# A small Pool memset behind each transfer of the landing-paced spreads in a four-layer mixture-of-experts kernel

## The chip, the cores and the metric

The kernel runs on 1 core of a Trainium2 chip. The metric is the device time of one launch in microseconds (us), given as the median of several runs; a profile of one further execution supplies the trace. The engines are TensorE (PE in the profile; PEld is its weight load), VectorE (DVE), ScalarE (ACT), GpSimd (POOL) and SyncE (SP, which here only issues transfers). Each has its own instruction stream and works it off in order. They wait for one another, and for transfers, by semaphores.

## The reference, cut to what matters

x has 4 sequences of 1024 tokens with 128 features, float32. It passes through four layers, each an attention-like mix and a feed-forward part, each with a residual and a layer norm behind it:

```python
x = L0_attn_x
x = _layernorm(x + _L0_attn_ref(x, ...))
x = _layernorm(x + _L0_ffn_ref(x, ...))     # a linear layer on block-quantised values
x = _layernorm(x + _L1_attn_ref(x, ...))    # a state-space mix
x = _layernorm(x + _L1_ffn_ref(x, ...))     # 16 experts, 4 for a token, and a shared one
x = _layernorm(x + _L2_attn_ref(x, ...))    # causal attention, 16 heads of 8
x = _layernorm(x + _L2_ffn_ref(x, ...))     # 8 experts, 2 for a token
x = _layernorm(x + _L3_attn_ref(x, ...))    # a Toeplitz mix, gated
x = _layernorm(x + _L3_ffn_ref(x, ...))     # 32 experts, 4 for a token, and a shared one
```

What matters here are the three expert parts. A router gives each token its k experts with a weight each:

```python
topk_scores, topk_idx = jax.lax.top_k(scores, TOPK)
...
h = silu(flat @ gate_w[e]) * (flat @ up_w[e])      # of each chosen expert e
expert_out = h @ down_w[e]
out = sum over the chosen e of expert_out * topk_scores
```

## The kernel before, in words

x stays on the chip in 32 tiles of 128 tokens. The kernel doesn't compute all experts for all tokens: it sorts the tokens by expert into lists in the chip's DRAM, in these steps.

- **Positions** (`positions`, L1261). For a set of tokens and a layer, DVE works out each token's row in the list for each of its choices (`pos`, L1302), so that every expert's rows stand together.
- **Spread** (`spread`, L1374). For each tile of 128 tokens and each choice, POOL issues one indirect transfer (L1327, in `indirect`) that writes the tile's 128 rows of 512 bytes to their places in the list. The lists are named by layer and set: l1r is layer 1's second list (64 transfers), l2a, l2m and l2n are layer 2's lists (32, 16, 16), l3a is layer 3's first (64). In the profile the list's own name has a letter more: l1rr, l2ra, l2rm, l2rn, l3ra.
- **Experts.** For each group of four tiles of a list, SP loads the rows (`gathered`, L1392: xg); this load waits until all transfers of that list have landed. PE transposes them (L169; the copies out are L171 on ACT and L173 on DVE, as hT for the hidden values) and multiplies (L161); DVE multiplies the two branches (L1569) and copies the result out (yg, L1589), and SP stores it to an output list (L1590).
- **Collect** (`collect`, L1439). POOL gathers each token's k results from the output list (yt, again L1327), and DVE adds them to x with their weights (L1452).

Every indirect transfer, scatter or gather, is queued on POOL behind the one before it (`self.moved`), so POOL works them off in one fixed order. Some spreads and collects are "spaced" (`spaced`, L1364): in them each transfer also waits until the transfer two before it has landed (`before`, L1346). All spreads named above are spaced. The first list of layer 1 and the two later lists of layer 3 are not; they issue their transfers without such waits.

The order between the engines' streams is set when the program is built. Parts of the kernel are generators that yield an estimated cost, and `mix` interleaves a main part with a side part by these costs; `self.now`, `self.step` and `self.moved_by` keep the planner's clock. Around the change, from `all` (L1966), the order is:

1. Layer 2's attention for the first half of its rows, with the route and spread of l1r beside it.
2. The experts and the shared expert of l1r, with layer 2's weights loading and the route and spread of l2a beside them. The weights of the shared expert lie in buffers that xg uses later.
3. Layer 2's experts on l2a, with the collect of l1r (64 gathers) beside them.
4. Layer 2's attention for the other half. Beside it: the collect of l2a, layer 3's mix and route for its first set, and the spread of l3a, into which those of l2m and l2n are put when their rows are ready. l3a is issued as 32 transfers, then l2n's 16, then 32 more; l2m's 16 come before.
5. Layer 2's experts on l2m; then on l2n, with the collect of l2m (16 gathers, list l2ym) beside them. These gathers stand behind the last transfers of l3a on POOL.
6. Layer 3's shared part and experts, with the rest beside them.

The functions the diff touches:

Of the kernel before, what the change touches and what calls it, by code (L numbers as in the profile page):

```python
# [20 lines left out]
P = 128  # L21
# [35 lines left out]
class Part:  # L57
# [3 lines left out]
    def __init__(self, name, q0, nq, rows=None, lg0=None):  # L61
        self.name, self.q0, self.nq, self.lg0 = name, q0, nq, lg0
        if rows is None:
            self.order = list(range(q0 * QT, (q0 + nq) * QT))
        else:
            self.order = [tile_of(b, 2 * q + k) for b in rows for q in range(q0, q0 + nq) for k in range(2)]
        self.t0, self.nt = q0 * QT, len(self.order)
# [7 lines left out]
class Kernel:  # L75
    def __init__(self, ctx, tc, ins, out, cols, consts, rows):
        self.tc, self.nc, self.ins, self.out = tc, tc.nc, ins, out
        self.count = itertools.count()
        nc = self.nc
        self.const = self.pool(ctx, "const")  # L80
        self.small = self.pool(ctx, "small", 3)
        self.routes = self.pool(ctx, "routes")
        self.side = self.pool(ctx, "side", 2, space=PSUM)
        dram = self.pool(ctx, "dram", space=DRAM)

        self.cols_t = self.load(self.const, ins["cols"])
        self.cst_t = self.load(self.const, ins["consts"])
        self.x = self.tile(self.const, [P, NT, D], "x")
        self.xT = self.tile(self.const, [P, NT * P], "xT")
        nrow = ins["rows"].shape[1]  # L90
        self.rows_t = self.tile(self.const, [P, nrow], "rows")
        nc.gpsimd.dma_start(out=self.rows_t, in_=ins["rows"].to_broadcast([P, nrow]))
        self.col = {k: self.cols_t[:, a:b] for k, (a, b) in cols.items()}
        self.cst = {k: self.cst_t[:, a:b] for k, (a, b) in consts.items()}
        self.row = {k: self.rows_t[:, a:b] for k, (a, b) in rows.items()}
        self.ident = self.cst["ident"]
        self.eps = self.tile(self.const, [P, 1], "eps")
        nc.vector.memset(self.eps, LN_EPS)
        self.halfpi = self.tile(self.const, [P, 1], "halfpi")
        nc.vector.memset(self.halfpi, math.pi / 2)  # L100
        self.ones = self.tile(self.const, [P, E3], "ones")
        nc.vector.memset(self.ones, 1.0)
        self.rnd = self.tile(self.const, [P, 1], "rnd")
        nc.vector.memset(self.rnd, RND)
        self.drop = self.tile(self.const, [P, 1], "drop")
        nc.vector.memset(self.drop, -RND)
        self.zero = self.tile(self.const, [P, D], "zero")
        nc.gpsimd.memset(self.zero, 0.0)
        self.flag = self.tile(self.const, [1, 1], "flag", I32)
        self.hm = self.tile(self.const, [P, 4], "hmg")  # L110

        self.first, self.rest = Part("a", 0, 2), (Part("b", 2, 1), Part("c", 3, 1))
        self.parts = (self.first, *self.rest)
        self.by_rows = (
            Part("a", 0, 2, range(B), 0), Part("m", 2, 2, (0, 1), NT // 2), Part("n", 2, 2, (2, 3), 3 * NT // 4)
        )

        self.rows_done = 0

        self.listed = set()  # L120

        self.traced, self.latest = nc.cur_bb.bb.instructions, {}
        self.now = self.moved_by = 0.0
        self.moved = []
        self.landing = []
        self.spacing = None

        self.lists, self.route = {}, {}
        self.both = (self.first, Part("r", 2, 2))
        for lay, ne, k in (("l1", E1, K1), ("l2", E2, K2), ("l3", E3, K3)):  # L130
            for pt in {"l1": self.both, "l2": self.by_rows, "l3": self.parts}[lay]:
                tl = -(-((pt.nt * P * k + (P - 1) * ne) // P) // 4) * 4
                self.lists[lay, pt.name] = (
                    self.tile(dram, [tl * P, D], f"{lay}r{pt.name}"), self.tile(dram, [tl * P, D], f"{lay}y{pt.name}"), tl
                )
        self.wall2 = self.tile(dram, [P, E2 * 3 * F2], "wall2")
        self.xsave = self.tile(dram, [P, NT, D], "xsave")

        self.ksave = self.tile(dram, [P, B, BLK], "ksave")
        self.vsave = self.tile(dram, [P, B, 4, (NH + 1) * VW], "vsave")  # L140
# [1232 lines left out]
    def spread(self, lay, part, k):  # L1373

        pos, _, _, done, _ = self.route[lay + part.name]
        rows = self.lists[lay, part.name][0]
        for t in range(part.nt):
            for i in range(k):
                ins = self.indirect(
                    apart=done,  # L1380
                    out=rows, out_offset=bass.IndirectOffsetOnAxis(ap=pos[:, t, i : i + 1], axis=0),
                    in_=self.x[:, part.order[t], :], in_offset=None,
                )
                done.append(ins)
            yield (self.step * k,)
        self.listed.add(lay + part.name)

# [835 lines left out]
```

## Time and profile before

| | us |
|---|---|
| median of 3 runs | 1932.44 (1931.96 to 1936.04) |
| the profiled execution | 1937.33 |
| its span in the trace | 1935.5 |
| PE busy | 1541.5 |
| DVE busy | 1199.2 |
| ACT busy | 900.6 |
| POOL busy | 690.3 |

The granted clock of TensorE over this execution is 0.896 of full speed.

In the profile, a row of a timeline gives the start, the busy time, the engine, the line, the operation with what it writes and reads, how often it ran in a row, and in brackets the engine's idle time before it and what ended that. A row of a group gives the busy time in sum and the mean of one instruction in ns, then the idle time before the group's instructions and its causes. In the windows, each stretch has the busy time of PE, PEld, DVE, ACT and POOL (with instruction counts), then the granted clock, the share of time in which DMA engines worked, and GB/s. L numbers are lines of the kernel before. SPq is SP's queue.

### The profile page before, as it was taken

The page shows a single profiled execution, that of the slowest core. Times are in us where ns is not written, and L with a number is a line of the kernel's source. Part 1 is how long each engine was busy: PE and PEld are TensorE (multiplying, and loading weights), DVE is VectorE, ACT ScalarE, POOL GpSimd, SP SyncE. Part 2 cuts the span into 40 slices and gives each one's busy share as a digit, 9 for nine tenths or more (in the row PEclk, how much of TensorE's full clock was granted, in tenths as well). Part 3 has the DMA queues.
Part 4 walks back from the last instruction along what each step waited for, and adds up shares of the span by engine and source line. Part 5 has one row for each costly group of instructions (what it writes and reads, how often), then busy time and mean ns, then how long its engine had stood idle before and what let it go on. Part 6 is the DMA issues. An engine that isn't in the chain of part 4 may idle for free. (4 is left out here: it accounts for less than half of the span.)

```text
span 1935.5 us, 27095 instructions
## 1 busy us (share of the span) xinstructions
PE 1541.5 (80%) x9025; PEld 920.8 (48%) x9025; DVE 1199.2 (62%) x3491; ACT 900.6 (47%) x1349; POOL 690.3 (36%) x670
## 2 busy tenths in 40 slices
PE   7885677597847887989977878798798998999850
PEld 3332433385423345856632232333355757768650
DVE  8998698465766664635564565546442446866383
ACT  5876265243324554423336756564532236644330
POOL 2000148604630660265443000030536430567775
PEclk9897688798978998999988988898988999989985
DMA  9990002244430113632241000000452213425452
GB/s 297 288 288 10 1 17 86 87 126 133 159 129 18 60 63 129 183 96 73 78 137 32 1 1 1 2 23 1 159 213 83 66 28 93 141 68 167 122 147 61
DMA packets 215530, 187.10 MB, mean 97 GB/s; under 512 B 16528, under 2 KB 194064, under 8 KB 214864
## 3 DMA queue, kind: packets, MB, share of 16 engines
q1 hardware_dynamic: 194672, 142.29, 23.6%
q0 software_dynamic: 20704, 42.86, 7.3%
q8 instruction: 84, 1.38, 0.3%
q14 instruction: 70, 0.57, 0.1%
HBM read 88.49 MB, written 96.60 MB: 96 GB/s over the span
## 5 line engine op out<-in xcount | busy, mean ns | idle before, releaser
L1081 ACT ACTIVATE pr<-sc 128x1024 f32<-128x1024 f32 x288 | 279.4, 1021 | 175.2 <-PE sc L161 174.8
L161 PE MATMUL sc<-qm,kT 32*128 32x512 f32 (+3 forms) x1536 | 197.7, 559 | 16.7 <-ACT pr L1081 16.7
L161 PE MATMUL s<-pr,va 128*32 128x512 f32 (+3 forms) x1536 | 167.5, 532 | 19.0 <-DVE x L1019 10.2
L161 PE MATMUL gu<-ld,xgT 128*128 x640 | 165.1, 400 | 10.2 <-DVE hg L1812 5.9
L1087 DVE TENSOR_TENSOR pr<-pr,ld 128x512 f32<-128x512 f32 (+1 forms) x160 | 91.7, 581 | 105.6 <-ACT pr L1081 105.4
L161 PE MATMUL gu<-wall,xgT 128*128 x304 | 148.2, 612 | 2.0 <-ACT xgT L171 2.0
L161 PEld LDWEIGHTS sc<-qm,kT 32*128 32x128 f32 x1536 | 83.7, 194 | 112.4 <-issue 61.1
L161 PEld LDWEIGHTS gu<-ld,xgT 128*128 128x128 f32 x640 | 119.5, 198 | 34.7 <-DVE hg L1812 6.1
L1812 DVE TENSOR_TENSOR hg<-sg,gu 128x256 f32<-128x256 f32 x160 | 66.0, 417 | 92.0 <-ACT sg L1811 91.6
L173 DVE COPY hT<-tp 128x512 f32<-128x512 f32 x118 | 80.9, 686 | 66.2 <-PE tp L169 66.2
L1567 ACT ACTIVATE sg<-gu 128x512 f32<-128x512 f32 x76 | 45.4, 597 | 144.7 <-PE gu L161 143.6
L1811 ACT ACTIVATE sg<-gu 128x256 f32<-128x256 f32 x160 | 61.3, 385 | 107.7 <-PE gu L161 79.8
L171 ACT COPY xgT<-tp 128x512 f32<-128x512 f32 x99 | 58.0, 586 | 99.9 <-PE tp L169 99.8
L1327 POOL DMA_INDIRECT l1ra<-x,posl1a x64 | 79.8, 1246 | 61.3 <-DVE peq L1321 42.0
L1327 POOL DMA_INDIRECT l1rr<-x,posl1r x64 | 65.4, 1022 | 100.9 <-DVE posl1r L1302 70.8
L169 PEld LDWEIGHTS tp<-ld,hg 128*128 128x128 f32 x624 | 77.4, 141 | 49.0 <-issue 32.5
L1569 DVE TENSOR_TENSOR hg<-sg,gu 128x512 f32<-128x512 f32 x76 | 51.8, 682 | 78.9 <-ACT sg L1567 78.8
L1327 POOL DMA_INDIRECT l2rm<-x,posl2m x16 | 15.7, 983 | 236.8 <-DVE peq L1320 230.1
L169 PE MATMUL tp<-ld,hg 128*128 128x128 f32 x624 | 96.4, 275 | 3.7 <-DVE hg L1812 2.0
L1327 POOL DMA_INDIRECT l3ra<-x,posl3a x64 | 63.7, 996 | 93.3 <-DVE usedl3a L1315 51.0
L161 PEld LDWEIGHTS s<-pr,va 128*32 128x32 f32 x1536 | 37.1, 113 | 122.6 <-issue 78.4
L161 PE MATMUL yp<-ld,hT 128*128 x640 | 86.1, 276 | 2.3 <-DVE mv L197 1.5
(447 smaller groups left out, 3439.1 us busy)
## 6 DMA issues: line engine op xcount, KB each, us to landing
wall<-wall SPq DMA_DIRECT2D x16, 768.0 KB, 7.8
l3ra<-zero SPq DMA_DIRECT2D x1, 6144.0 KB, 25.5
ld<-in_l_w SPq DMA_DIRECT2D x2, 3072.0 KB, 10.6
wall<-we SPq DMA_DIRECT2D x24, 256.0 KB, 2.1
ld<-in_l_w SPq DMA_DIRECT2D x1, 6144.0 KB, 20.6
l1ra<-zero SPq DMA_DIRECT2D x1, 5120.0 KB, 19.6
l1rr<-zero SPq DMA_DIRECT2D x1, 5120.0 KB, 23.1
xg<-l3ra SPq DMA_DIRECT2D x20, 256.0 KB, 2.9
```

What stands on the lines that cost most here:

```text
L161: return self.nc.tensor.matmul(out, lhsT, rhs, start=start, stop=stop)
L169: nc.tensor.transpose(pt[:, k * P : (k + 1) * P], s, self.ident)
L171: nc.scalar.copy(dst, pt[:, : n * P])
L173: nc.vector.tensor_copy(dst, pt[:, : n * P])
L1081: nc.scalar.activation(pr, sc[h], AF.Exp)
L1087: nc.vector.tensor_tensor(d, d, cst["tril"].unsqueeze(1).unsqueeze(1).to_broadcast([P, 2, n, P]), ALU.mult)
L1327: ins = self.nc.gpsimd.indirect_dma_start(**kw)
L1567: nc.scalar.activation(sg, gu[:, 0, :], AF.Silu)
L1569: nc.vector.tensor_tensor(h, sg, gu[:, 1, :], ALU.mult)
L1811: nc.scalar.activation(sg, pg[:, :, 0, :], AF.Silu)
L1812: nc.vector.tensor_tensor(h[:, 2 * c : 2 * c + 2, :], sg, pg[:, :, 1, :], ALU.mult)
```

## The change

One tile of 128x384 bytes is added to the constants, and in `spread`, when the spread is spaced, a memset of it on POOL follows each indirect transfer. The memset is ordered behind the transfer on POOL's stream and entered in `self.moved`, so that the next indirect transfer is ordered behind the memset. It doesn't wait for the transfer's landing, and nothing reads the tile. The waits for landings stay. In all it adds 192 memsets: 64 for l1r, 32 for l2a, 16 each for l2m and l2n, 64 for l3a. The planner's costs are not changed, and the streams of the other engines have the same instructions in the same order.

```diff
         self.eps = self.tile(self.const, [P, 1], "eps")
+        self.idle = self.tile(self.const, [P, 384], "idle", mybir.dt.uint8)
         nc.vector.memset(self.eps, LN_EPS)
...
                 done.append(ins)
+                if self.spacing:
+                    stay = self.nc.gpsimd.memset(self.idle, 0)
+                    self.tc.add_manual_dep(
+                        stay.ins, ins.ins.name,
+                        mybir.DependencyInfo(mybir.DependencyClass.NoSync, mybir.DependencyReason.DATA),
+                        reason="queued behind",
+                    )
+                    self.moved.append(stay.ins.name)
             yield (self.step * k,)
```

## The prediction

> **What bounds the kernel.** I read the page's first part, the costliest groups, then timelines around the consumer of each changed spread.
>
> ```profile
> PE 1541.5 (80%) x9025; PEld 920.8 (48%) x9025; DVE 1199.2 (62%) x3491; ACT 900.6 (47%) x1349; POOL 690.3 (36%) x670
> L1327 POOL DMA_INDIRECT l1rr<-x,posl1r x64 | 65.4, 1022 | 100.9 <-DVE posl1r L1302 70.8
> ```
>
> TensorE sets the pace (80%); POOL is busy for 36% of the span, nearly all in scatters and gathers. A slower POOL costs nothing until a list lands later than the first group of tokens (xg) could be loaded from it, or until whatever is queued behind a spread on POOL is late. So I ask of each spread how much longer it gets, and what then comes late.
>
> ```profile
> 805.14 0.95 POOL L1327 DMA_INDIRECT l2ra<-x,posl2a  x1 [80.52 <-DVE posl2a L1302]
> 806.39 0.96 POOL L1327 DMA_INDIRECT l2ra<-x,posl2a  x1 [0.30 <-issue]
> 808.67 0.96 POOL L1327 DMA_INDIRECT l2ra<-x,posl2a  x1 [1.32 <-DMA l2ra<-x,posl2a]
> 809.94 0.95 POOL L1327 DMA_INDIRECT l2ra<-x,posl2a  x1 [0.30 <-issue]
> ```
>
> A transfer holds POOL for 0.96 us and the next one starts 0.30 later: 1.26 us apiece. Now and then it must wait for the landing of the transfer two before (1.32 in the third row). POOL starts of each spread, added up from the timeline:
> - l1rr, 63 steps: 94.6 us, of which 11.0 are waits beyond the 0.30 (11 of them)
> - l2ra, 31: 49.3, waits 10.2 (11)
> - l2rm, 15: 21.5, waits 2.2 (2)
> - l3ra, first half, 31: 57.4, waits 15.9 (14)
> - l2rn, 15: 34.9, waits 16.0 (5)
> - l3ra, second half, 31: 45.9, waits 6.8 (9)
>
> **The price m of one memset.** The change adds 192 memsets (64+32+16+16+64), on POOL alone; the order on PE, DVE, ACT and SP stays as it was. No row shows 128x384 bytes on POOL. The nearest:
>
> ```profile
> L344 POOL MEMSET keep<- 128x1024 f32 x1 | 1.0, 955 | 0.0
> L108 POOL MEMSET zero<- 128x128 f32 x1 | 0.2, 232 | 0.0
> ```
>
> ```profile
> 1.99 0.23 POOL L108 MEMSET zero<- 128x128 f32 x1
> 2.14 0.58 POOL L271 DMA_DIRECT2D taps<-in_taps  x1
> ```
>
> The groups give (955-232)/896 = 0.81 ns an element. By reported durations 384 elements take 0.232+256x0.00081 = 0.44, with a start some 0.48 us. But the next instruction started 0.15 after the 128-element memset, while it reports 0.23. The Trainium skill ("Perfetto Trace Analysis", GPSIMD Engine Instruction) holds GpSimd spans unreliable and would go by the spacing of consecutive starts: 0.145+256x0.00081 = 0.35. By spacing the sum below is +8 us, by durations +16. I take the spacing, m = 0.36, since starts are also what the cadence was read from. Against any slowdown stands a rule in "VectorE: DVE Perf Modes", Zero memsets can be issued as uint32: a zero memset of bytes may be written in 4-byte words, a quarter of the elements. Then these are 96 elements, m = 0.12 (0.145 less 32x0.00081), and the sum is nothing. The page says it of the Vector engine; the trace has only f32 memsets on POOL, so no row decides, and the program holds 384 one-byte elements. I keep 0.12 and 0.48 as ends. Below 0.12 is possible if the 0.30 between transfers hides the memset.
>
> **How a spread grows.** Each step gains m; but a transfer waits for one issued two steps, so two memsets, earlier, so each wait shrinks by up to 2m (0.72). Wait by wait:
> - l1rr: 63x0.36 = 22.7, waits give back 6.7: +16.0
> - l2ra: 11.2 less 6.5: +4.6
> - l2rm: 5.4 less 1.4: +4.0
> - l3ra first half: 11.2 less 7.7: +3.5
> - l2rn: 5.4 less 3.6: +1.8
> - l3ra second half: 11.2 less 4.7: +6.5
>
> For m = 0.12: +4.9, 1.2, 1.3, 0.5, 0.6, 1.6; for 0.48: +22.5, 7.0, 5.5, 5.5, 2.4, 9.5. Whether a memset on POOL holds up a DVE instruction beside it, no row shows. DVE, at 62%, has room in these stages, so I put that at nothing; at worst an instruction of DVE on the path is late by one m, 0.36 us, now and then.
>
> **Where it costs nothing.** l1rr ends its issue at 723.65; plus 16.0 and a landing of 2.2 it is 741.9, before its first xg at 745.48, which waits for the end of the attention on PE (at m = 0.48: 748.4, still ahead of PE's first use at 756.3). l2rm and the first half of l3ra end well before POOL's next gate, the positions of n at 1423.0 (POOL idles 10.9 us before it). l2rn lands 1.8 later, at about 1462, while its xg is issued at 1476.35 behind a store: 14 us of slack. l3ra's own xg comes at 1596.
>
> **Site A, behind l2ra.**
>
> ```profile
> 859.60 3.05 SPq L1392 DMA_DIRECT2D xg<-l2ra  x2
> 860.41 1.83 PE L161 MATMUL py<-ld,hs 128*128 128x128 f32 x14 [0.63 <-DVE hs L764]
> 862.58 0.63 PE L169 MATMUL tp<-ld,xg 128*128 128x128 f32 x4 [0.34 <-DMA xg<-l2ra]
> ```
>
> The last of the 32 transfers starts at 854.42 and lands at 856.6. The load of xg starts at 859.60, held until then by PE, which still reads the weights that lie in its buffer. So there are 3.0 us of slack; PE waits for xg only 0.34 but has no work left to cover more. With +4.6 the landing is 861.3: the load and PE are late by 1.7 us (0 at m = 0.12, 4.0 at 0.48). Behind l2ra on POOL are the gathers of layer 1's second list (64). They take over the 4.6 us, but POOL idles 9.15 us and 8.38 us among them (at 894 and 955) waiting for DVE's adds, so the lag ends there.
>
> **Site B, behind l3ra's second half.** Queued behind it are the 16 gathers of l2ym (L1327), whose sums (L1452) sit in DVE's order between the expert's own work.
>
> ```profile
> 1529.70 2.18 DVE L1452 SCALAR_TENSOR_TENSOR x<-yt,wkl2m,x 128x128 f32<-128x128 f32 x8
> 1531.80 0.68 DVE L173 COPY hT<-tp 128x512 f32<-128x512 f32 x1
> 1532.40 0.68 DVE L1569 TENSOR_TENSOR hg<-sg,gu 128x512 f32<-128x512 f32 x1
> 1532.99 1.13 DVE L1452 SCALAR_TENSOR_TENSOR x<-yt,wkl2m,x 128x128 f32<-128x128 f32 x4
> 1534.98 0.69 DVE L1569 TENSOR_TENSOR hg<-sg,gu 128x512 f32<-128x512 f32 x1 [0.85 <-ACT sg L1567]
> 1535.58 0.73 DVE L1452 SCALAR_TENSOR_TENSOR x<-yt,wkl2m,x 128x128 f32<-128x128 f32 x2
> 1537.83 0.69 DVE L173 COPY hT<-tp 128x512 f32<-128x512 f32 x1 [1.52 <-PE tp L169]
> ```
>
> The first gather starts at 1508.57, the last at 1531.44. They slide by 1.8 (l2rn) + 6.5 (l3ra) less about 0.5 of longer gaps between the lists, which a memset fills: +7.8. The last then starts at 1539.2, lands 2.6 later at 1541.8, and its two adds (0.73) end at 1542.6. DVE comes to the hT copy (L173) not at 1537.83 but about 4.8 later, and PE, in order, waits for hT. What this site absorbs is some 3 us; at m = 0.12 the slide of 2.2 fits, at 0.48 it costs 8.5.
>
> **The clock.** A PE idle of about 3 us has a price beyond itself:
>
> ```profile
> 785.00:788.40 3.40, 3.12 (x11) 2.74 (x12) 1.92 (x20) 0.59 (x1) 0.00 (x0) 0.50 0.58 168
> 836.20:843.00 6.80, 5.76 (x7) 2.52 (x8) 0.69 (x1) 0.86 (x2) 5.09 (x6) 0.50 0.31 103
> ```
>
> Both stretches (the column after POOL's is the granted clock) run at half clock, 3.4 us after an idle of 3.0 and 6.8 after one of 4.5; idles of 2.4 showed none. Half of 3.4, 1.7 us, is added at site B; twice that at m = 0.48.
>
> **The sum.** A 1.7 + B 4.8 + clock 1.7 = +8.2 us. The profiled execution took 1937.33 (span 1935.5 and 1.8 around it), so it would be 1945.5. It lies 4.9 above the median of the three runs; the same 8.2 on the median 1932.44 gives 1940.6.
>
> **Rivals.** *The price fits in the slack: not slower.* If the memset is written in words or lies in the 0.30 between transfers, l2ra grows by 1.2 or less, under the 3.0 of site A, and the gathers slide by 2.2, under the 3 of site B. The time stays 1932.4; up to 3 us may be won where fewer transfers crowd one load (the load of xg from l2rn takes 3.9 against 2.9 usually, and a half-clock stretch follows): 1929.5. It decides up to m of about 0.2; from there the two slacks are used up. For it: the rule on words, and the 0.15 spacing. Against: the program's 384 elements and the slope of 0.81 ns. *The memset is dearer than counted*, 0.48 or more: 4.0+8.5+3.4 = +15.9, 1948.3. For it: the reported 232 and 955 ns. *The delay is taken up behind the sites:* after A, PE works on a chain of experts whose weights may be what waits next, and at B another wait of PE (5.4 us for xg of l2rn, 5.7 for DVE at L213) may shrink. Then some half remains: 1936.5.
>
> **Chances.** Forecast 0.42, all slower; fits in the slack 0.28 (same 0.19, faster 0.09); dearer 0.14; taken up behind 0.12 (slower 0.07, same 0.05); a gain by spacing that I don't see in the rows 0.04. Within 0.2%, 3.9 us, the measurement can't tell a change from none. Faster 0.13, same 0.24, slower 0.63. The range runs from 1931.5, a little under no change, to 1950.0, above the dear memset; left out are the larger gains (0.1) and a memset over 0.5 us (0.1).
>
> **What would show it.** The starts of l2ra's transfers: 1.62 us apart where nothing waits, if m is 0.36; 1.26 to 1.38 for the rival, 1.74 for the dear one. l1rr's spread longer by 16 us without a later xg. The load of xg from l2ra issued when the last landing comes, near 861, with PE's idle before L169 grown from 0.34 to 2. At site B, the last gather 8 us later, PE waiting 4 to 5 us for hT. The forecast is wrong if the steps grow by under 0.2 us, or if the sites show their delays and the end of the span doesn't move.

## The result, and the profile after

The changed kernel takes 1948.55 us (median of 8 runs, 1940.35 to 1958.16), the kernel before, run beside it, 1932.63 (8 runs). The ratio is 1.0082 with a 95% interval of 1.0063 to 1.0100, so it is slower by 15.8 us (12 to 19). The prediction said slower, by 8.2 us, 1940.6, with a range to 1950.0: the direction is right and the time lies in the range, but close to its upper end, where the prediction had put the dear memset. (Some line numbers of the description are off: `spaced` begins at L1363, `spread` at L1373, `collect` at L1441 and `all` at L1957.)

The profiled execution took 1940.35 us, with a span of 1938.4. That is the fastest of the eight, while the profiled execution of before was the slowest of its own. So the two spans differ by only 2.9 us, and the traces are compared stage by stage and with the further traces below. The page after has these lines for the two shown of before (an inserted line shifts the line numbers by 1, behind `spread` by 9):

```profile
PE 1539.6 (79%) x9025; PEld 924.1 (48%) x9025; DVE 1205.3 (62%) x3491; ACT 899.6 (46%) x1349; POOL 772.4 (40%) x862
L1328 POOL DMA_INDIRECT l1rr<-x,posl1r x64 | 64.1, 1002 | 85.3 <-DVE posl1r L1303 70.9
```

POOL has 192 more instructions and 82.1 us more work; DVE has the same 3491 instructions and 6.1 us more busy time. That second number was not in the prediction.

Next the groups and POOL's timeline at the start of l2ra's spread, after:

```profile
L1387 POOL MEMSET idle<- 128x384 uint8 x192 | 84.0, 437 | 0.1
```

```profile
810.03 0.97 POOL L1328 DMA_INDIRECT l2ra<-x,posl2a  x1 [74.79 <-DVE posl2a L1303]
811.00 0.43 POOL L1387 MEMSET idle<- 128x384 uint8 x1
811.60 0.97 POOL L1328 DMA_INDIRECT l2ra<-x,posl2a  x1 [0.17 <-issue]
812.57 0.43 POOL L1387 MEMSET idle<- 128x384 uint8 x1
813.77 0.96 POOL L1328 DMA_INDIRECT l2ra<-x,posl2a  x1 [0.77 <-DMA l2ra<-x,posl2a]
```

A step that waits for nothing is 1.57 us (810.03 to 811.60) where it was 1.26. So m is 0.31, although the memset reports 0.44: the gap before the next transfer shrinks from 0.30 to 0.17. The third transfer still waits for a landing, but 0.77 in place of 1.32.

Then site A, after. The load of xg is now issued when the last landing comes, and PE waits for it:

```profile
862.48 0.96 POOL L1328 DMA_INDIRECT l2ra<-x,posl2a  x1 [0.17 <-issue]
864.84 4.34 SPq L1401 DMA_DIRECT2D xg<-l2ra  x3
864.87 1.83 PE L162 MATMUL py<-ld,hs 128*128 128x128 f32 x14 [0.63 <-DVE hs L765]
868.16 0.63 PE L170 MATMUL tp<-ld,xg 128*128 128x128 f32 x4 [1.46 <-DMA xg<-l2ra]
```

The last transfer starts at 862.48, the load 2.36 later. PE's idle time before the transposes is 1.46 where it was 0.34.

### The profile page after: what moved, and what is told of

It reads as the page before. It is cut to its first block, busy times and chain, and to the rows that moved or that the text cites. A ratio compares the mean times of both kernels' runs of the same rounds, so it can differ in the third digit from the quotient of the medians.

```text
span 1938.4 us, 27285 instructions
## 1 busy us (share of the span) xinstructions
PE 1539.6 (79%) x9025; PEld 924.1 (48%) x9025; DVE 1205.3 (62%) x3491; ACT 899.6 (46%) x1349; POOL 772.4 (40%) x862
## 5 line engine op out<-in xcount | busy, mean ns | idle before, releaser
L162 PE MATMUL gu<-ld,xgT 128*128 x640 | 166.3, 403 | 10.2 <-DVE hg L1821 5.9
```

The source lines that it names most:

```text
L162: return self.nc.tensor.matmul(out, lhsT, rhs, start=start, stop=stop)
```

## The experiments

The first four variants ran on one chip beside 29 runs of the kernel before, which have a median of 1930.41 us and lie between 1925 and 1937. The ratio given for each is an estimate with a 95% interval; the microseconds behind it are this ratio's part of 1930.41. They are not quite the differences of the medians, which are 7.2, 1.5 and 5.0 for the three parts.

**all_again**: the changed kernel, nothing edited but a tag.

> The changed kernel once more, with all 192 memsets. Every theory expects the measured +16 us again (1944 to 1953), with steps of l2ra that don't wait 1.57 us apart. The three runs beside it should add up to it. If the one profile of the changed kernel had a lucky clock in layer 2's second attention, this trace shows a lead of some 10 us over the kernel before kept to the end, and not 3 us.

Measured: 1947.55 us, ratio 1.0088 (1.0064 to 1.0112), +17.0 us. Its span is 1945.1, so this trace shows a typical execution. Compared instruction by instruction on ACT, its lag behind the kernel before is not constant: it is -5 us at about 640, up to +6 at 914, -0.6 at 1490 in front of site B and 7 to 10 behind it. Only the end is as expected.

**only_l1r, only_l2a, only_l2mn_l3a**: the condition alone is edited, to one list or one group of lists.

```diff
-                if self.spacing:
+                if lay + part.name in ('l1r',):
```

> Memsets behind the 64 transfers of l1r alone. The theory on record: its list lands 3 us before it is needed, so nothing: 1932.6, within 1 us. The rival, that DVE's tensor_scalar instructions are held up while POOL works, and that attention beside the spread waits for them: +3 to +5 us, 1936 to 1938, with DVE's busy time between 590 and 745 us up by 6 to 7 us, all of it in tensor_scalar, and the other stages as before.

Measured: 1937.63 us, ratio 1.0029 (1.0016 to 1.0042), +5.6 us. The prediction's view falls: memsets whose list lands in good time cost a third of the whole.

> Memsets behind the 32 transfers of l2a alone. On record: the load of xg from l2ra late by 1.7 us, so +1.7: 1934.3. The rival: the later gathers and experts behind it carry the lag on and PE's clock falls once more: +4 to +6, 1937 to 1939. If the load of xg isn't late at all: 1932.6.

Measured: 1931.95 us, ratio 1.0017 (1.0004 to 1.0031), +3.3 us (0.8 to 6.0). This is too wide to tell 1.7 from 4. Eight of its twelve runs lie at 1929 to 1933 and four at 1936 to 1940; the trace is of one of the eight (1929.34). In it PE's wait for xg is 1.1 us, and 1.46 and 1.9 in the two traces with all memsets, where it was 0.34: 0.8 to 1.6 us more are seen at the site.

> Memsets behind the 96 transfers of l2m, l2n and l3a. On record: the gathers of l2ym are 7.8 us late, DVE comes to hT 4.8 late, with 1.7 for the clock +6.5: 1939.1. The rival, that the memsets are shorter than counted (0.31 and not 0.36) and that the adds leave more room: +2 to +3, 1935.

Measured: 1935.39 us, ratio 1.0028 (1.0016 to 1.0040), +5.4 us (3.1 to 7.7). The prediction's +6.5 lies in this interval.

5.6 + 3.3 + 5.4 = 14.3, against 17.0 for all_again beside them: the three parts add up to the whole within their intervals.

**What l1r's memsets do.** The groups of DVE's tensor_scalar instructions between 600 and 765 us (count, sum in us, mean in ns) in the kernel before:

```profile
L213 DVE TENSOR_SCALAR x<-x,mv,rstd 128x128 f32<-128x128 f32 x16 | 4.5, 366 | 0.1
L964 DVE TENSOR_SCALAR qm<-qT,hmg 128x512 f32<-128x512 f32 x8 | 3.5, 498 | 0.1
L186 DVE TENSOR_SCALAR nwt<-nwt 128x4 f32<-128x4 f32 x12 | 2.2, 180 | 0.4
L204 DVE TENSOR_SCALAR ve<-mv 128x4 f32<-128x4 f32 x4 | 0.7, 170 | 0.1
```

and with memsets for l1r alone:

```profile
L214 DVE TENSOR_SCALAR x<-x,mv,rstd 128x128 f32<-128x128 f32 x16 | 5.3, 483 | 0.1
L965 DVE TENSOR_SCALAR qm<-qT,hmg 128x512 f32<-128x512 f32 x8 | 4.9, 676 | 0.1
L187 DVE TENSOR_SCALAR nwt<-nwt 128x4 f32<-128x4 f32 x12 | 2.8, 231 | 0.4
L205 DVE TENSOR_SCALAR ve<-mv 128x4 f32<-128x4 f32 x4 | 1.2, 304 | 0.1
```

Each of these forms became longer, the mean of the masks (qm) from 498 to 676 ns. Instructions in a row overlap in their reported times, so the extra time is read from the sums: 0.8 + 1.4 + 0.6 + 0.5 = 3.3 us. DVE's whole work in this part of the program (the stretch shown below) grew from 98.5 to 102.5 us. In the timeline of only_l1r a block of four norms shows where it arises:

```profile
645.57 0.44 POOL L1387 MEMSET idle<- 128x384 uint8 x1
645.84 1.40 DVE L214 TENSOR_SCALAR x<-x,mv,rstd 128x128 f32<-128x128 f32 x4
646.18 0.96 POOL L1328 DMA_INDIRECT l1rr<-x,posl1r  x1 [0.17 <-issue]
647.14 0.44 POOL L1387 MEMSET idle<- 128x384 uint8 x1
```

The four take 1.40 us, where four in a row took 1.12 in the kernel before; they end (647.24) just behind the transfer (647.14). The tensor_tensor instructions with two operands, most of DVE's work in the stage, are not longer.

Over a whole trace, take each tensor_scalar that started 0.1 to 0.5 us into a transfer, and compare it with the shortest of its form (forms that occur at least four times). Directly behind a 384-byte memset it was 0.26 to 0.56 us longer: all 12 such in only_l1r, and 13 of 15 in the changed kernel's first trace. In the kernel before, none of 51 was more than 0.24 longer, and 45 of them less than 0.1. A tensor_scalar that started in the first 0.2 us of a 384-byte memset was 0.24 to 0.29 longer (5 of 5 in the first trace, 4 of 4 in only_l1r); behind or beside a 96-byte memset, in quarter_c, at most 0.16.

The Trainium skill ("SBUF — State Buffer", 🔬 SBUF: two separate sides) has a rule for it: an instruction of DVE in a two-port mode and one of GpSimd take a shared pair of ports for the whole instruction, and the other blocks. The rows agree that tensor_scalar is held up, but not that a transfer holds it for its whole length: in the kernel before, all 45 that started in the first 0.4 us of a transfer were at most 0.07 us longer.

The stage pays for it. The same stretch of the program, from one exp of the attention to the first group of l1r behind it, in the kernel before, in the changed kernel, and in quarter_c (below), which has 192 memsets of 96 bytes:

```profile
606.20:757.50 151.30, 121.23 (x1123) 61.01 (x1124) 98.51 (x346) 80.00 (x95) 65.44 (x64) 0.93 0.15 55
```

```profile
605.80:761.10 155.30, 119.48 (x1123) 60.68 (x1121) 103.14 (x346) 79.95 (x95) 92.27 (x128) 0.95 0.15 54
```

```profile
606.80:758.00 151.20, 118.68 (x1123) 61.27 (x1124) 98.73 (x346) 79.79 (x95) 78.10 (x128) 0.95 0.15 56
```

At the same granted clock of 0.95 the stretch takes 155.3 us with long memsets and 151.2 with short ones. The stretch differs by 4.1 us and DVE's busy time (third in each row) by 4.4; those of PE and ACT differ by less than 1. The waits of PE in this stretch (us in all, times, the longest), after:

```profile
PE s L170 <- DVE x L214: 9.4, 6, 5.5
PE s L162 <- DVE rot L955: 4.2, 4, 2.2
```

and in quarter_c:

```profile
PE s L170 <- DVE x L214: 7.3, 3, 5.5
PE s L162 <- DVE rot L955: 2.7, 4, 1.2
```

PE waits 2.1 us longer for the norm and 1.5 longer for the rotated queries (L955), which stand behind the masks on DVE. In all_again and only_l1r the stretch takes 160.8 and 161.4 at a clock of 0.88. Here PE's clock takes part. The second block of norms, in the kernel before and in only_l1r, and the clock behind it in only_l1r:

```profile
691.26 1.07 PE L169 MATMUL s<-ld,x 128*128 128x128 f32 x4 [0.81 <-DVE x L213]
```

```profile
687.21 0.60 PE L170 MATMUL s<-ld,x 128*128 128x128 f32 x2 [1.65 <-DVE x L214]
688.10 0.69 PE L170 MATMUL s<-ld,x 128*128 128x128 f32 x2 [0.30 <-DVE x L214]
```

```profile
687.50:697.70 10.20, 9.90 (x46) 3.90 (x45) 4.27 (x11) 4.04 (x5) 9.18 (x14) 0.50 0.10 39
```

PE waits for the norms 1.95 us in place of 0.81, and then runs 10.2 us at half clock; at the next block it waits 1.67 and 0.40 in place of 0.79, and 6.8 us at half clock follow (from 731.8). all_again has the same two. The other five traces at the usual speed have no half clock between 670 and 745, the changed kernel's first trace among them, although PE waited there as long (1.81 and 0.40). So the held norms can cost clock as well, but did not in each execution. The stretch also starts some 5 us earlier in all_again and only_l1r, after a stage in front of it with less half clock, so part of the loss only moved from there. Counted from before that, at 561 us, to 754, the three traces with l1r memsets lose 4.4, 6.7 and 7.0 us against the kernel before; the traces without (only_l2a, only_l2mn_l3a and quarter_c) lose -0.7, 1.8 and 1.8.

**The size of a memset: words, quarter, quarter_c.**

```diff
-        self.idle = self.tile(self.const, [P, 384], "idle", mybir.dt.uint8)
+        self.idle = self.tile(self.const, [P, 96], "idle", U32)
```

(words; quarter and quarter_c have [P, 96] of uint8.)

> All 192 memsets, each of 96 four-byte words in place of 384 bytes (the same bytes). If the time of a memset goes by elements: 0.21 us reported, steps of 1.33 to 1.36 without a wait, and a time of 1932 to 1940. If it goes by bytes: 0.43 and 1.57, and 1945 to 1952 as in the changed kernel.

> All 192 memsets, each of 96 bytes. By elements: the same as the run with words. By bytes: 0.15 us or less, steps of 1.3, and about the time before, 1932 to 1936. If each memset costs by holding up DVE however short it is, the time stays above 1940.

> 192 memsets of 96 bytes once more, to see them on a chip on which the kernel before takes about 1930 us. There: within 2 us of the kernel before, if the changed kernel's 16 us come with the length of its memsets (tensor_scalar held up, lists later by 0.31 us a step); +5 or more, if any memset costs. On a chip on which the kernel before takes about 2240: 1.0 to 1.3% below it, as twice measured.

The groups, of words and of quarter:

```profile
L1387 POOL MEMSET idle<- 128x96 uint32 x192 | 37.4, 195 | 2.6 <-remote 2.1
```

```profile
L1387 POOL MEMSET idle<- 128x96 uint8 x192 | 37.7, 196 | 0.1
```

A memset of 96 words and one of 96 bytes take the same 0.195 us, and in both the free step is 1.33 us, so m = 0.07. It goes by elements, not by bytes. (0.31-0.07)/288 = 0.83 ns an element, which is nearly the 0.81 of the prediction; and 384x0.81 is 0.31, so nothing comes on top of the elements.

quarter_c took 1932.03 us, ratio 1.0004 (0.9991 to 1.0018). As many memsets, a quarter as long, cost nothing that can be measured. In its trace the masks take 497 ns and the norms 355, as without memsets, and PE waits 0.49 us for l2ra's xg, where it was 0.34.

**The two sets with words, quarter, the other forms and quarter_b.** On the two chips that ran these sets the kernel before itself took 2235.28 and 2249.05 us, with a granted clock of about 0.85. So their times say nothing on the 16 us and are only listed; durations of single instructions in their traces are used. One of the two chips ran quarter_c later at the usual speed.

| run | median us | ratio to the kernel before beside it |
|---|---|---|
| words | 2209.91 | 0.9866 (0.9796 to 0.9936) |
| quarter | 2214.19 | 0.9875 (0.9815 to 0.9935) |
| other_form | 2245.30 | 1.0083 (1.0041 to 1.0126) |
| other_form_memset | 2140.63 | 0.9624 (0.9581 to 0.9668) |
| no_fast | 2259.12 | 1.0132 (1.0034 to 1.0230) |
| no_fast_l1r | 2209.14 | 0.9821 (0.9711 to 0.9932) |
| quarter_b | 2214.85 | 0.9895 (0.9796 to 0.9994) |

Whatever slowed these executions, those with memsets lost less by it: here memsets made the kernel faster, from 2245.30 to 2140.63 between other_form and other_form_memset. Part of it can be seen. Beside l1r's spread ACT once stands still for 43.8 us in other_form's trace, and for 33.1 in no_fast's; in other_form_memset and no_fast_l1r, with 384-byte memsets in this spread, its longest idle time there is 7.9, as in the kernel before at the usual speed. What holds ACT is not shown, and nothing below rests on it.

**other_form, other_form_memset, no_fast, no_fast_l1r**: tensor_scalar written in other forms, two of its places in the first pair, four in the second.

```diff
-                nc.vector.tensor_scalar(x, x, mv[:, t, 0:1], rstd[:, t : t + 1], ALU.subtract, ALU.mult)
+                nc.vector.scalar_tensor_tensor(
+                    x, x, mv[:, t, 0:1], rstd[:, t : t + 1].to_broadcast([P, D]), ALU.subtract, ALU.mult,
+                )
...
-                        nc.vector.tensor_scalar(qm[:, m, :], qT, self.hm[:, m : m + 1], None, ALU.mult)
+                        nc.vector.tensor_tensor(qm[:, m, :], qT, self.hm[:, m : m + 1].to_broadcast([P, BLK]), ALU.mult)
```

> No memsets; two of DVE's tensor_scalar instructions, in the norm (L213) and in the heads' masks (L964), are written as scalar_tensor_tensor and tensor_tensor. The base for the next run. A mask is some 0.2 us longer, 32 of them are 7 us of DVE, partly on the path: 1932 to 1940. If instructions of these forms are not held up by POOL, none of them shows more than 0.1 us above its shortest.

> The same with all 192 memsets. If holding up DVE's tensor_scalar is a large part of the cost: only +8 to +12 us over the run without memsets, where the changed kernel lost 16, and DVE's busy time between 590 and 745 us up by under 2 us. If it is no part of the cost: +16 again.

> No memsets; four of DVE's tensor_scalar instructions (L186, L204, L213, L964) are written as tensor_tensor or scalar_tensor_tensor. The base for the next run: the masks are some 0.2 us longer each, so 1930 to 1938 on a chip whose kernel before takes 1930.

> The same with memsets behind the 64 transfers of l1r. If these memsets cost time (5.6 us with tensor_scalar) because POOL holds up tensor_scalar on DVE: 0 to 2 us over the run without memsets, and DVE's busy time between the start of l1r's spread and its end up by less than 2 us, from the few tensor_scalar that are left. If they cost through the later landing or through the transfers themselves: 5 to 6 us again.

> All 192 memsets of 96 bytes, whose steps were 0.07 us longer. By the sum of the prediction for m = 0.12 the lists stay inside the slack of both sites, and the traces showed tensor_scalar held up no more than without memsets: within 2 us of the kernel before. If the cost came with the number of memsets and not with their length: +10 or more.

None of the times expected here can be judged. The durations can. In other_form none of the masks and norms in their new forms is more than 0.06 us above the shortest of its form, as expected. Between 640 and 860 us, no_fast has

```profile
L968 DVE TENSOR_TENSOR qm<-qT,hmg 128x512 f32<-128x512 f32 x8 | 5.0, 686 | 0.1
L215 DVE SCALAR_TENSOR_TENSOR x<-x,mv,rstd 128x128 f32<-128x128 f32 x12 | 3.4, 348 | 0.4 <-DVE rstd L189 0.3
L182 DVE TENSOR_SCALAR rstd<-ve 128x4 int32<-128x4 int32 x3 | 0.5, 170 | 0.1
```

and no_fast_l1r:

```profile
L969 DVE TENSOR_TENSOR qm<-qT,hmg 128x512 f32<-128x512 f32 x8 | 5.0, 686 | 0.1
L216 DVE SCALAR_TENSOR_TENSOR x<-x,mv,rstd 128x128 f32<-128x128 f32 x16 | 4.6, 348 | 0.1
L183 DVE TENSOR_SCALAR rstd<-ve 128x4 int32<-128x4 int32 x4 | 1.2, 304 | 0.1
```

With 384-byte memsets beside them, the mask in its new form stays at 686 ns and the norm at 348. The tensor_scalar that was left as it was goes from 170 to 304. So the form of DVE's instruction decides whether POOL holds it up. (The groups of the norm have 12 and 16 because the windows cut the program at different places.)

The stretch shown above for the stage beside l1r's spread ran in no_fast_l1r without ACT's long idle times and at the same clock of 0.95, so it can be set beside the others; that of no_fast cannot:

```profile
647.90:803.80 155.90, 120.37 (x1123) 61.62 (x1121) 101.08 (x346) 79.95 (x95) 94.34 (x128) 0.95 0.15 54
```

It takes 155.9 us, no less than the 155.3 of the changed kernel. PE no longer waits longer for the norms: 5.5 us for them and 1.8 for the step in front of them (nwt), against 7.3 in quarter_c. But the new forms make DVE's work longer too: it is 100.2 us in no_fast and 98.7 in quarter_c, and the new masks are as long as the held ones. DVE's 101.1 explains 2.4 of the 4.7 us over quarter_c; the rest is not explained.

## Why the prediction was right, and where half of it was missing

**The price m: right.** It said 0.36 by the spacing of starts, with 0.12 and 0.48 as ends; 0.31 was measured. The choice of spacing over reported duration was right (0.44 is what the memset reports). The skill's step from bytes to words is one that a program takes, and this one doesn't take it: its 384 one-byte elements ran as 384. Written as words (words) they cost what 96 elements cost, but 0.07 a step where the prediction had 0.12.

**How the spreads grow: right but for the smaller m.** After less before: l1rr +10.6 us (said +16.0), l2ra +3.2 (4.6), l2rm +4.8 (4.0), l3ra's halves +3.1 and +5.0 (3.5 and 6.5), l2rn +1.6 (1.8). Longer steps did shorten the waits for landings.

**Site A: right, but for the clock.** The load of xg was late because of the last landing, and PE waited 1.1 to 1.9 us for it, where 2 was said. The prediction charged no clock here. Behind the wait, in the changed kernel's first trace, stands

```profile
870.40:873.80 3.40, 3.40 (x5) 1.35 (x4) 0.69 (x1) 0.60 (x1) 1.76 (x2) 0.50 0.33 90
```

that is 3.4 us at half clock, as in all_again (from 868.1); the kernel before and only_l2a have none there. The prediction charged the clock for idles of about 3 us, since those of 2.4 showed none. But in the kernel before the half-clock stretches at 1204.9 and 1638.4 come with idles of PE of only 1.8.

**Site B: right, but for the clock.** The prediction's two numbers there, a slide of 7.8 and some 3 us absorbed, can be compared with three traces. DVE's timeline in all_again:

```profile
1538.44 0.35 DVE L1461 SCALAR_TENSOR_TENSOR x<-yt,wkl2m,x 128x128 f32<-128x128 f32 x1 [0.75 <-DMA yt<-l2ym,posl2m]
1541.20 0.61 DVE L1461 SCALAR_TENSOR_TENSOR x<-yt,wkl2m,x 128x128 f32<-128x128 f32 x2 [2.41 <-DMA yt<-l2ym,posl2m]
1543.55 0.35 DVE L1461 SCALAR_TENSOR_TENSOR x<-yt,wkl2m,x 128x128 f32<-128x128 f32 x1 [1.73 <-DMA yt<-l2ym,posl2m]
1543.82 0.68 DVE L1578 TENSOR_TENSOR hg<-sg,gu 128x512 f32<-128x512 f32 x1
1544.65 0.35 DVE L1461 SCALAR_TENSOR_TENSOR x<-yt,wkl2m,x 128x128 f32<-128x128 f32 x1
1546.36 0.35 DVE L1461 SCALAR_TENSOR_TENSOR x<-yt,wkl2m,x 128x128 f32<-128x128 f32 x1 [1.36 <-DMA yt<-l2ym,posl2m]
1546.63 0.68 DVE L174 COPY hT<-tp 128x512 f32<-128x512 f32 x1
```

DVE stands in its order waiting for one gather after the other, and the hT copy that was at 1537.83 comes at 1546.63. With the offset at which each trace entered the stage taken off, the last add slid by 11.0 us in all_again, 8.4 in only_l2mn_l3a and 2.9 in the changed kernel's first trace; the copy of yg that is at 1541.78 in the kernel before came 7.7, 5.2 and 0.0 later. Each time some 3 us are absorbed, as said. The half-clock stretch that the prediction added is there in all_again (3.4 us from 1537.1), and not in the other two. How far the gathers slide differs from execution to execution, and that may be one reason for the wide spread of the changed kernel's times (1940 to 1958).

**The step that failed** reads: "Whether a memset on POOL holds up a DVE instruction beside it, no row shows. DVE, at 62%, has room in these stages, so I put that at nothing". And so l1r stood under "where it costs nothing". The runs gave +5.6 us (3.1 to 8.1) for l1r's memsets alone. Its list did land in time, 13 us ahead of its first load; the cost came by another way, through some 40 tensor_scalar instructions on DVE, a few tenths each, on which PE waits for the attention's next operands. DVE's share over the whole span said nothing on this: the norm, the rotation and the masks stand in a row in front of PE. The prediction's own bound for it ("late by one m, 0.36 us, now and then") allowed for one and not for a sum: the means of norms and masks rose by 0.12 to 0.18. The prediction came out right because it got the direction and two of three places; its range reached far enough for the third, which it did not foresee.

So the sum: A and the clock and B were put at 8.2 us; the two runs that hold them gave 3.3 + 5.4 = 8.7. The missing term is l1r's 5.6. Together 14.3, of 17.0 in all_again and 15.8 in the first measurement. That 8.7 comes so near to 8.2 is in part luck: the clock's term lay at another site in part, and each of the two runs is known to some 2 us only.

**What is shown and what is argued.** That the memsets for l1r cost 5.6 us is shown, that tensor_scalar is held up is shown, and that short memsets do neither. That the hold-ups are all of the 5.6, by themselves and by the clock behind them, is argued from the stretch at equal clock (4.1 us, DVE +4.4, PE's waits for DVE +3.6) and not shown. The run that was to show it, no_fast_l1r, ran where times can't be compared, and its stretch, with the norms no longer held, is as long as the changed kernel's; about 2 us of that have no explanation. How some 1 us at A becomes 3.3 is open too: half of the 3.4 us at half clock would be 1.7 more, but only_l2a's own trace has no half clock there.

**The rivals.** "The price fits in the slack" had its bound right: at m = 0.07 nothing is lost, at 0.31 both sites are over. "Dearer", with 1948.3, has the right time for a wrong reason: the memset is not dearer, there is a third place where it costs. "Taken up behind" isn't seen in the parts. A gain by spacing was seen only in the two sets at 2240 us.

## What to carry to other kernels

Work on an engine that is idle for most of the span isn't free: before putting work on GpSimd, look for tensor_scalar instructions of DVE in the same stretch, and whether another engine waits for them, list by list and not by DVE's share. A delay in a stream costs what it slides beyond the slack, and of two late lists the one with work queued behind it on the same engine is the dear one. If a pause between transfers is wanted, its length decides: 0.07 us a transfer was free here, 0.31 cost 16 at the kernel's usual speed.

## What the runs showed of the hardware

- A zero memset on POOL goes by elements, about 0.83 ns each: 96 words and 96 bytes both report 0.195 us and lengthen a step by 0.07; 384 bytes report 0.437 and lengthen it by 0.31.
- A transfer directly behind a 384-byte memset holds a tensor_scalar of DVE that starts 0.1 to 0.5 us into it for 0.26 to 0.56 us; one without a memset mostly not, and for at most 0.24 us. The transfer's own 0.96 us doesn't change. Whether it is the memset, past its reported end, or the transfer that holds DVE isn't shown.
- tensor_tensor and scalar_tensor_tensor, in place of the same tensor_scalar, are not held: 686 and 348 ns with and without memsets.
- Medians of the same kernel were 1930 to 1933 us in three sets of runs and 2235 to 2249 in two; one chip showed both speeds. In the slow sets a memset behind each transfer made it faster.
